# First expert tiles of a fused attention and expert block: numbers in one woven part, weights asked in halves, ScalarE's table loaded ahead

## The chip, the cores and the metric

The kernel runs on one core of a Trainium2 chip. The metric is the device time of one execution in microseconds. The core has five engines that each run their own list of instructions in order: TensorE (PE) for matrix products, VectorE (DVE) and ScalarE (ACT) for work on vectors, GpSimd (POOL) for odd jobs and indirect transfers, and SyncE (SP), which here only issues DMA transfers. The engines wait for each other through semaphores.

## The reference

The input `x` has shape (2, 2048, 256): 4096 tokens. The reference is one block of a network, cut here to what is computed:

```python
# attention: a gated linear recurrence on the normalized input
n   = layernorm(x)
v   = n @ W_write.T                            # 4 heads of 64
rk  = n per head;  wk = rk shifted by one token
# per chunk of tokens: read from the state W, read inside the chunk, write to the state
inter = W @ rk * gamma**p ;  intra = ((rk @ wk.T) * M) @ v
W     = gamma**C * W + (v * g_w).T @ wk
x   = x + n + (alpha * reads) @ W_read.T
# experts: 8 of them, the best two for each token
n   = layernorm(x)
p   = softmax(n @ gate_w.T);  top 2 experts e with weights p_e
h   = gelu(w1[e] @ n + b1[e])                  # 256 -> 1024, tanh approximation
x   = x + sum over e of p_e * (w2[e] @ h + b2[e])
```

## The kernel before

The attention goes in 16 chunks `p` of 128 tokens in both batch rows (`attention(p)`). For each chunk, PE makes `pv` (values and gate columns, line 413), `pS` (products inside the chunk, line 422), `pO` (the result of the chunk before, line 391), the transposes `pt` of the next chunk (line 340), and the reads `pR` (lines 465 and 473) and state writes `pW` (line 493). DVE multiplies `pS` by the mask to give `A` (line 428), adds `pO` to the rows (line 394), updates the state (line 498) and makes `rg` (line 353). ACT copies `pv` to `v` (line 415), scales `wkg` and copies `yT`.

Two chunks make a group `q` of 512 tokens (two chunks in each of the two batch rows), eight groups in all. When a group's rows are done, `route(q)` finds the top two experts of each token and the place in a DRAM table `slots` for it. POOL writes the rows there with eight indirect transfers (`to_slots`). Then `dispatch(q)` finds which experts have a further full tile of 128 rows, and where each such tile starts. Its numbers `t_e` (the expert) and `t_row` (the first row) are computed on DVE by a dozen small operations, in `whole` and around it. `EARLY` fixes the counts: 9 tiles after group 1, 8 after each of groups 2 to 6, and the rest after group 7. 67 tiles run in any case, and four spare ones only if needed.

An expert tile is eight pieces (`piece`). A piece is a product `ph` with a slice of the expert's first weights `w1c` (line 851), a GELU on ACT that gives `hT` (line 856), and three pieces later a product `py` with the second weights, which stay in SBUF (line 813). Before the first piece `prepare` transposes the tile's rows `xg` on PE into `px` (line 787), copies them on DVE to `xT` (line 789), and fetches the bias `b1c`. `px` and `pt` use the same single PSUM buffer with the tag `pt`. `ph` and `pv` use the three buffers `pm`.

SP fetches for a tile the bias row `b2c` (line 755), the weights `w1c` (1 MiB, line 757) and the rows `xg` (line 767). For each it first reads `t_e` or `t_row` into a register (line 746), and so waits until DVE has written it. `w1c`, `b2c` and `xg` have four buffers each.

All engines run in the order in which the Python code issues the instructions. The generators decide the order: `attention(p)` yields at seven steps `k`, and at each the main loop lets `advance` move the routing on. A routing generator that yields `1` asks to be continued by `beside()`, one operation at a time, between the operations of the attention on DVE. A plain `yield` ends its part at this step, and it goes on at the next. Pieces of expert tiles begin in chunk 9 by `pieces_by`.

The main loop asks for weights at each step by `ask_weights_on(stream["piece"] // FC + 2)`, so for the first two tiles as soon as their numbers are known, and at a chunk's end for rows by `ask_on(stream["piece"] // FC + 3)`, so for three tiles. Later, `piece` asks for tile `t + 3` at the second piece of tile `t`.

Of the kernel before, what the change touches and what calls it, by code (L numbers as in the profile page):

```python
# [10 lines left out]
F32 = mybir.dt.float32  # L11
I32 = mybir.dt.int32
AF = mybir.ActivationFunctionType
# [5 lines left out]
P = 128  # L19
B, T, D = 2, 2048, 256  # L20
H, HD = 4, 64
E, F = 8, 1024
# [4 lines left out]
FC = F // P  # L27
# [19 lines left out]
def block_kernel(  # L47
# [16 lines left out]
    nc = tc.nc  # L64
# [11 lines left out]
    def one(shape, dt, name):  # L76
        return keep.tile(shape, dt, name=name)
# [33 lines left out]
    ident = one([P, P], F32, "ident")  # L111
    make_identity(nc, ident)
    nc.gpsimd.memset(ones, 1.0)
    expo = one([P, G], F32, "expo")
    nc.gpsimd.memset(expo, -0.5)
    age = iota(one([P, P], F32, "age"), [[1, P]], -1, -1)
# [105 lines left out]
    def wide(t, k):  # L222
        return t.unsqueeze(2).to_broadcast([P, t.shape[1], k])

    def by_e(t, n):
        return t.unsqueeze(1).to_broadcast([P, n, t.shape[1]])
# [32 lines left out]
    EASY = 9  # L259
    BUSY = 8  # L260
# [266 lines left out]
    def route(q):  # L527
# [105 lines left out]
        yield 1  # L633
        nc.vector.tensor_tensor(pay[:, :, D : D + E], pr, ohs[:, :G], ALU.mult)
        numbers = dispatch(q) if q < NG - 1 else dispatch_rest()
        for k in range(2):
            for i in range(G):
# [9 lines left out]

    tiles, found, known = [], [], []

    def whole(n_f, n, name, ef, row, pick):  # L650

        upto = sml.tile([P, E], F32, tag="upto", name=f"upto_{name}")
        sofar = sml.tile([P, E, E], F32, tag="sofar", name=f"sofar_{name}")
        nc.vector.tensor_tensor(sofar, by_e(n_f, E), not_over, ALU.mult)
        yield 1
        nc.vector.tensor_reduce(upto, sofar, AX.X, ALU.add)
        yield
        origin = sml.tile([P, E], F32, tag="origin", name=f"origin_{name}")
        nc.vector.tensor_tensor(origin, upto, n_f, ALU.subtract)
        yield 1  # L660
        nc.vector.scalar_tensor_tensor(origin, origin, -float(SB), taken, ALU.mult, ALU.add)
        yield 1
        tmp = sml.tile([P, n, E], F32, tag=f"tmp{n}", name=f"tmp_{name}", bufs=1)
        nc.vector.tensor_tensor(tmp, wide(jj[:, :n], E), by_e(upto, n), ALU.is_ge)
        yield 1
        nc.vector.tensor_reduce(ef, tmp, AX.X, ALU.add)
        yield 1
        nc.vector.tensor_tensor(pick, wide(ef, E), by_e(e_of, n), ALU.is_equal)
        yield
        nc.vector.tensor_tensor(tmp, pick, by_e(origin, n), ALU.mult)  # L670
        yield 1
        first = sml.tile([P, n], F32, tag=f"first{n}", name=f"first_{name}", bufs=1)
        nc.vector.tensor_reduce(first, tmp, AX.X, ALU.add)
        yield 1
        nc.vector.scalar_tensor_tensor(row, jj[:, :n], float(SB), first, ALU.mult, ALU.add)

    def dispatch(q):

        n = EARLY[q]
        if not n:  # L680
            return
        n_i = sml.tile([P, E], I32, tag="n_i", name=f"n_i_{q}")
        n_f = sml.tile([P, E], F32, tag="n_f", name=f"n_f_{q}")
        nc.vector.tensor_tensor(n_i, carry[0], taken, ALU.subtract)
        yield 1
        nc.vector.tensor_scalar(n_i, n_i, SB.bit_length() - 1, None, ALU.logical_shift_right)
        yield 1
        nc.vector.tensor_copy(n_f, n_i)
        yield
        t_e = one([P, n], I32, f"t_e_{q}")  # L690
        t_row = one([P, n], I32, f"t_row_{q}")
        hot = one([P, n, E], F32, f"hot_{q}")
        ef = sml.tile([P, n], F32, tag=f"ef{n}", name=f"ef_{q}", bufs=1)
        yield from whole(n_f, n, str(q), ef, t_row, hot)
        nc.vector.tensor_copy(t_e, ef)
        yield
        got = sml.tile([P, E], F32, tag="got", name=f"got_{q}")
        nc.vector.tensor_reduce(got, hot.rearrange("p n e -> p e n"), AX.X, ALU.add)
        yield 1
        nc.vector.scalar_tensor_tensor(taken, got, float(SB), taken, ALU.mult, ALU.add)  # L700
        found.extend((t_e[0:1, j : j + 1], t_row[0:1, j : j + 1], hot[:, j, :], q) for j in range(n))
        known.extend(found)

    def dispatch_rest():
# [14 lines left out]
        nc.vector.tensor_copy(needed, total)  # L719
        ef, row, hot = one([P, NMAX], F32, "ef"), one([P, NMAX], F32, "row"), one([P, NMAX, E], F32, "hot")  # L720
        yield from whole(n_f, NMAX, "rest", ef, row, hot)
        yield

# [17 lines left out]
    stream = {"weights": 0, "asked": 0, "piece": 0, "last": NTILE - SPARE}  # L741
# [3 lines left out]
    def load(src, engine, most):  # L745
        _, (value,) = nc.values_load_multi_w_load_instructions(
            src, [engine], min_val=0, max_val=most, bass_reorder=False
        )
        return value

    def ask_weights(t):

        ev = load(known[t][0], ENG.SP, E - 1)
        b2c = tok.tile([P, D], F32, tag="b2c", name=f"b2c_{t}", bufs=4)
        nc.sync.dma_start(b2c, b2[ds(ev, 1), :].to_broadcast([P, D]))
        w1c = tok.tile([P, 2, F], F32, tag="w1c", name=f"w1c_{t}", bufs=4)
        nc.sync.dma_start(
            w1c.rearrange("p c f -> p (c f)"), w1.rearrange("e p n -> (e p) n")[ds(ev * P, P), :]
        )
        got[t] = (b2c, w1c)  # L760

    def ask(t):

        _, row_at, _, q = tiles[t]
        r0 = load(row_at, ENG.SP, DUMMY)
        xg = tok.tile([P, ROW], F32, tag="xg", name=f"xg_{t}", bufs=4)
        behind(nc.sync.dma_start(xg, next(slot_views)[ds(r0, SB), :]), up_to(q, filled))
        got[t] = (xg, *got[t])

    def ask_weights_on(upto):  # L770
        while stream["weights"] < min(upto, len(known), stream["last"]):
            ask_weights(stream["weights"])
            stream["weights"] += 1

    def ask_on(upto):
        while stream["asked"] < min(upto, len(tiles), stream["last"]):
            ask_weights_on(stream["asked"] + 1)
            ask(stream["asked"])
            stream["asked"] += 1
# [112 lines left out]
    def behind_first():  # L892

        next(setup)
        for c in range(2):
            nc.vector.tensor_scalar(wrg[:, c, :D], wrg[:, c, :D], alpha[:, c : c + 1], None, ALU.mult)
        nc.sync.dma_start(slots[DUMMY : DUMMY + SB, :], empty)
        nc.sync.dma_start(out[N : N + SB, :], empty[:, :D])
        nc.sync.dma_start(b1_sb, b1)

    STEPS = 7
    def advance(whole=True):

        for r in list(routing):
            while inside.get(r) == 1:
                onward(r)
            if r in routing:
                onward(r)
            while whole and inside[r] == 1:
                onward(r)  # L910

    def pieces_by(p, k):


        n = 0.0
        for q, count in enumerate(EARLY):
            share = (p * STEPS + k + 1 - (2 * q + LATE) * STEPS) / (2 * STEPS)
            n += count * FC * min(max(share, 0), 1)
        return int(n)
# [6 lines left out]
    def gate_products():  # L926
# [6 lines left out]
        for m in range(2):  # L933
            nc.vector.tensor_scalar(wrg[:, m, D:], pg[:, m, :], alpha[:, m : m + 1], None, ALU.mult)

    for p in range(NC):
        for k, _ in enumerate(attention(p)):
            if p == 0 and k == 0:
                behind_first()
            if (p or k > 3) and k in (0, 2, 3, 4, 5) and halves < W2_BY[p]:  # L940
                e, j = divmod(halves, 2)
                js = slice(j * FC * D // 2, (j + 1) * FC * D // 2)
                nc.sync.dma_start(w2_sb[:, e, js], w2[e, :, js])
                halves += 1
            if p % 2 == 0 and p and k == 2:
                routing.insert(0, route(p // 2 - 1))
            todo = pieces_by(p, k) - stream["piece"]
            if p < BUSY or not todo:
                advance(p > EASY)
            ask_weights_on(stream["piece"] // FC + 2)  # L950
            for i in range(todo):
                piece()
                if p >= BUSY and (i % 2 == 0 or i == todo - 1):
                    advance()
        if p % 2 and p >= BUSY:
            while routing:
                advance()
        ask_on(stream["piece"] // FC + 3)
    for _ in result(NC - 1):
        piece()  # L960
    routing.append(route(NG - 1))
# [66 lines left out]
```

## Time and profile before

| | |
|---|---|
| median of 3 runs | 642.66 us (640.2 to 644.68) |
| profiled execution | 662.17 us |
| its span, first to last instruction | 660.2 us |
| mean granted clock of TensorE | 0.98 |
| busy: PE, DVE, ACT, POOL | 627.8, 263.3, 287.3, 223.7 us |
| moved by DMA | 129.77 MB |

The profile is of one execution, and its times stand against that execution's own 662.17 us. A group of instructions is named by line, engine, operation and tiles (written tile, arrow, read tiles). In the timeline each row has a start and a length in us; in brackets stands the time that the engine was idle before it, and what ended that. "issue" there means that the profile shows nothing that the engine waited for, "remote" that a semaphore ended the wait and its author isn't known. The chunks can be told by `pv` on PE: chunk 6 begins at 58.92, chunk 7 at 66.47, chunk 8 at 77.57, chunk 9 at 86.81 us.

### The profile page before, as it was taken

How to read it: one execution, taken by the hardware profiler on the slowest of the kernel's cores; microseconds unless marked ns; L12 is line 12 of the kernel's file. 1: busy time of each engine (PE TensorE's matmuls, PEld its weight loads, DVE VectorE, ACT ScalarE, POOL GpSimd, SP SyncE). 2: the span in 40 equal slices, each digit the busy share in tenths (PEclk: the TensorE clock that was granted, in tenths of full speed). 3: DMA queues.
4: the chain of work that ended last, by engine and by line, in shares of the span. 5: the costliest groups of instructions: out<-in, count | busy, mean ns of one | idle time of the engine just before them, and what ended most of it. 6: DMA issues, size and time to landing. Idle time of an engine off the chain costs nothing. (4 is left out here: it accounts for less than half of the span.)

```text
span 660.2 us, 15051 instructions
## 1 busy us (share of the span) xinstructions
PE 627.8 (95%) x4734; PEld 569.2 (86%) x4734; DVE 263.3 (40%) x1138; ACT 287.3 (44%) x769; POOL 223.7 (34%) x199
## 2 busy tenths in 40 slices
PE   7998869899999999999999969999999999999994
PEld 7877659798999898999999959999999999999994
DVE  5788766325543365425542532221122212112220
ACT  6776743334434353434433413444444444444441
POOL 4225483415641165214541551112112211221221
PEclk9999889999999999999999979999999999999998
DMA  4899694866776656677676668767866776666641
GB/s 133 260 332 302 197 319 115 243 177 190 176 215 186 188 151 205 202 192 191 162 203 180 203 198 215 214 184 199 209 205 187 209 215 186 189 225 201 185 99 19
DMA packets 58736, 129.77 MB, mean 197 GB/s; under 512 B 7984, under 2 KB 43952, under 8 KB 50080
## 3 DMA queue, kind: packets, MB, share of 16 engines
q1 hardware_dynamic: 45232, 111.16, 55.6%
q0 software_dynamic: 12720, 17.47, 12.5%
q8 instruction: 42, 0.69, 0.4%
q14 instruction: 38, 0.31, 0.2%
q10 hardware_dynamic: 704, 0.14, 0.1%
HBM read 101.54 MB, written 23.01 MB: 189 GB/s over the span
## 5 line engine op out<-in xcount | busy, mean ns | idle before, releaser
L851 PEld LDWEIGHTS ph<-xT,w1c 128*128 128x128 f32 x2144 | 319.8, 193 | 38.2 <-issue 10.8
L851 PE MATMUL ph<-xT,w1c 128*128 128x128 f32 x2144 | 331.5, 278 | 12.1 <-issue 9.9
L856 ACT ACTIVATE hT<-ph,b1c 128x128 f32<-128x128 f32 x536 | 195.9, 367 | 306.3 <-PE ph L851 278.3
L813 PE MATMUL py<-w_sb,hT 128*128 x1072 | 321.7, 383 | 0.0
L820 POOL DMA_INDIRECT out<-yo,dest x67 | 105.1, 1568 | 328.2 <-DVE dest L803 81.3
L813 PEld LDWEIGHTS py<-w_sb,hT 128*128 128x128 f32 x1072 | 164.2, 193 | 0.2
L819 DVE SCALAR_TENSOR_TENSOR yo<-py,wt,b2c 128x256 f32<-128x256 f32 x67 | 32.3, 483 | 248.7 <-PE py L813 241.7
L521 POOL DMA_INDIRECT slots<-pay,slot_i x64 | 63.4, 990 | 54.6 <-ACT hT L856 19.5
L413 PE MATMUL pv<-wwg,yT 128*128 128x264 f32 x128 | 34.0, 410 | 1.9 <-DVE yT L343 1.2
L391 PE MATMUL pO<-wrg,rdT 128*128 128x264 f32 x128 | 33.3, 393 | 0.4 <-issue 0.4
L428 DVE TENSOR_TENSOR A<-pS,dmask 128x1024 f32<-128x1024 f32 x16 | 19.6, 1224 | 35.3 <-PE pS L422 19.2
L413 PEld LDWEIGHTS pv<-wwg,yT 128*128 128x128 f32 x128 | 24.4, 197 | 6.8 <-DVE yT L343 1.4
L789 DVE COPY xT<-px 128x256 f32<-128x256 f32 x67 | 27.8, 415 | 1.5 <-remote 1.1
L391 PEld LDWEIGHTS pO<-wrg,rdT 128*128 128x128 f32 x128 | 23.6, 190 | 5.1 <-issue 0.8
L394 DVE TENSOR_TENSOR x<-x,pO 128x264 f32<-128x264 f32 x32 | 13.4, 426 | 33.4 <-PE pO L391 30.7
L787 PE MATMUL px<-ident,xg 128*128 128x128 f32 x134 | 25.9, 276 | 0.7 <-ACT yT L346 0.7
L801 DVE TENSOR_SCALAR b2c<-b2c,wt 128x256 f32<-128x256 f32 x67 | 24.9, 372 | 2.5
L787 PEld LDWEIGHTS px<-ident,xg 128*128 128x128 f32 x134 | 18.9, 142 | 7.5 <-ACT yT L346 0.9
L473 PE MATMUL pR<-A,v 128*64 128x128 f32 x256 | 18.6, 279 | 3.1 <-issue 2.2
L232 POOL TENSOR_TENSOR rstd_a<-ve_a,expo 128x2 f32<-128x2 f32 x16 | 13.1, 819 | 23.2 <-DVE ve_a L230 13.7
L422 PEld LDWEIGHTS pS<-yT 64*128 64x128 f32 x256 | 15.5, 187 | 5.8 <-issue 3.8
L551 ACT ACTIVATE pay<-x,shift_b,rstd_b 128x256 f32<-128x256 f32 x32 | 19.0, 594 | 2.4 <-DVE shift_b L237 2.3
(162 smaller groups left out, 431.7 us busy)
## 6 DMA issues: line engine op xcount, KB each, us to landing
w1c<-in_w SPq DMA_DIRECT2D x67, 1024.0 KB
xg<-slots SPq DMA_DIRECT2D x67, 132.5 KB
b2c<-in_b SPq DMA_DIRECT2D x67, 128.0 KB
w_sb<-in_w SPq DMA_DIRECT2D x16, 512.0 KB
out<-x SPq DMA_DIRECT2D x16, 256.0 KB
xin<-in_x SPq DMA_DIRECT2D x15, 256.0 KB
wk<-y SPq DMA_DIRECT2D x16, 224.0 KB
slots<-empty SPq DMA_DIRECT2D x9, 132.5 KB
```

The source lines that it names most:

```text
L391: nc.tensor.matmul(pO, lhsT=rdTs[p][:, c, b * P : (b + 1) * P], rhs=wrg[:, c, :], start=(c == 0), stop=(c == 1))
L413: nc.tensor.matmul(pv, lhsT=yT[:, b, c, 1:], rhs=wwg[:, c, :], start=(c == 0), stop=(c == 1))
L428: nc.vector.tensor_tensor(A, pS.rearrange("p j (b g) -> p j b g", b=B), dmask.rearrange("p j g c -> p j (g c)").unsqueeze(2).to_broadcast( ...
L521: put = nc.gpsimd.indirect_dma_start(out=next(slot_views), out_offset=IndirectOffsetOnAxis(ap=index, axis=0), in_=rows, in_offset=None,)
L787: nc.tensor.transpose(px[:, c, :], xg[:, c * P : (c + 1) * P], ident)
L789: nc.vector.tensor_copy(xT, px)
L801: nc.vector.tensor_scalar(b2c, b2c, wt, None, ALU.mult)
L813: nc.tensor.matmul(r["py"], lhsT=hT, rhs=w2_sb[:, ds(r["at"], 1), fc * D : (fc + 1) * D].rearrange("p a d -> p (a d)"), start=(fc == 0), s ...
L819: nc.vector.scalar_tensor_tensor(yo, r["py"], r["wt"], r["b2c"], ALU.mult, ALU.add)
L820: add = nc.gpsimd.indirect_dma_start(out=next(out_views), out_offset=IndirectOffsetOnAxis(ap=r["dest"], axis=0), in_=yo, in_offset=None, c ...
L851: nc.tensor.matmul(ph, lhsT=r["w1c"][:, c, fc * P : (fc + 1) * P], rhs=r["xT"][:, c, :], start=(c == 0), stop=(c == 1),)
L856: mark[0] = nc.scalar.activation(hT, ph, AF.Gelu_apprx_tanh, bias=r["b1c"][:, fc : fc + 1]).ins.name
```

## The change

There are three edits.

First, `dispatch(q)` and `whole` yield `pause` where they yielded plainly. `pause` is `1` while `2 * (q + 1) < EASY`, so for groups 1 to 3; the numbers of these groups are then issued in one part, one operation at a time beside the attention's, as far as that has places, and the rest at once.

Second, the first two tiles' weights are asked by a generator, `bits`. At each step without pieces it takes one part: the register load and `b2c`, then one half of `w1c`, then the other, and the same for the second tile. While no piece has run, only the rows of two tiles are asked at a chunk's end and not of three.

Third, at step 5 of chunk 7 ACT runs a GELU on one element, so that its table is loaded there.

```diff
+    table = one([1, 1], F32, "table")
...
-    def whole(n_f, n, name, ef, row, pick):
+    def whole(n_f, n, name, ef, row, pick, pause=None):
...
         nc.vector.tensor_reduce(upto, sofar, AX.X, ALU.add)
-        yield
+        yield pause
...
         nc.vector.tensor_tensor(pick, wide(ef, E), by_e(e_of, n), ALU.is_equal)
-        yield
+        yield pause
...
+        pause = 1 if 2 * (q + 1) < EASY else None
...
         nc.vector.tensor_copy(n_f, n_i)
-        yield
+        yield pause
...
-        yield from whole(n_f, n, str(q), ef, t_row, hot)
+        yield from whole(n_f, n, str(q), ef, t_row, hot, pause=pause)
         nc.vector.tensor_copy(t_e, ef)
-        yield
+        yield pause
...
     def ask_weights(t):
 
+        for _ in weights_of(t, 1):
+            pass
+
+    def weights_of(t, parts):
+
         ev = load(known[t][0], ENG.SP, E - 1)
         b2c = tok.tile([P, D], F32, tag="b2c", name=f"b2c_{t}", bufs=4)
         nc.sync.dma_start(b2c, b2[ds(ev, 1), :].to_broadcast([P, D]))
         w1c = tok.tile([P, 2, F], F32, tag="w1c", name=f"w1c_{t}", bufs=4)
-        nc.sync.dma_start(
-            w1c.rearrange("p c f -> p (c f)"), w1.rearrange("e p n -> (e p) n")[ds(ev * P, P), :]
-        )
         got[t] = (b2c, w1c)
+        n = 2 * F // parts
+        for i in range(parts):
+            yield
+            nc.sync.dma_start(
+                w1c.rearrange("p c f -> p (c f)")[:, i * n : (i + 1) * n],
+                w1.rearrange("e p n -> (e p) n")[ds(ev * P, P), i * n : (i + 1) * n],
+            )
...
+    def bits():
+        while not known:
+            yield
+        for t in range(2):
+            stream["weights"] += 1
+            yield from weights_of(t, 2)
+            yield
+
+    first_weights = bits()
     for p in range(NC):
         for k, _ in enumerate(attention(p)):
...
+            if p == BUSY - 1 and k == 5:
+
+                nc.scalar.activation(table, expo[0:1, 0:1], AF.Gelu_apprx_tanh)
...
-            ask_weights_on(stream["piece"] // FC + 2)
+            if stream["piece"] or todo:
+                for _ in first_weights:
+                    pass
+                ask_weights_on(stream["piece"] // FC + 2)
+            else:
+
+                next(first_weights, None)
...
-        ask_on(stream["piece"] // FC + 3)
+        if stream["piece"]:
+            ask_on(stream["piece"] // FC + 3)
+        elif tiles:
+            for _ in first_weights:
+                pass
+            ask_on(2)
```

## The prediction

> **What bounds the kernel now.** I read the busy lines of the page first. TensorE (PE) is busy 627.8 of 660.2 us, so only what keeps PE waiting, or its clock low, counts.
>
> ```profile
> PE 627.8 (95%) x4734; PEld 569.2 (86%) x4734; DVE 263.3 (40%) x1138; ACT 287.3 (44%) x769; POOL 223.7 (34%) x199
> ...
> PEclk9999889999999999999999979999999999999998
> ```
>
> The change works between chunk 6 of the attention and the first expert tiles, so next I cut that stretch into windows (columns: stretch, length, busy of PE, weight loads, DVE, ACT, POOL, then granted clock, DMA share, GB/s).
>
> ```profile
> 74.00:82.00 8.00, 6.17 (x52) 4.80 (x53) 6.10 (x30) 5.67 (x16) 1.22 (x3) 0.79 0.73 231
> 82.00:90.30 8.30, 8.30 (x94) 6.58 (x90) 7.71 (x39) 4.07 (x13) 6.04 (x7) 1.00 1.02 399
> 90.30:96.30 6.00, 0.05 (x2) 0.04 (x1) 1.82 (x4) 2.11 (x6) 5.06 (x5) 0.87 0.97 319
> 96.30:103.50 7.20, 7.20 (x34) 6.84 (x35) 4.22 (x21) 3.87 (x8) 4.37 (x2) 0.63 0.70 186
> ```
>
> PE stands still from 90.3 to 96.3, with the DMA engines full (0.97), and then runs at a clock of 0.63. The timeline tells what it waits for (start, length, engine, operation, idle before it and what ended that).
>
> ```profile
> 73.09 1.04 PE L473 MATMUL pR<-A,v 128*64 128x128 f32 x7
> 75.97 0.74 PE L473 MATMUL pR<-A,v 128*64 128x128 f32 x9 [1.83 <-issue]
> ...
> 89.88 0.44 PE L787 MATMUL px<-ident,xg 128*128 128x128 f32 x2
> 93.40 1.23 DVE L428 TENSOR_TENSOR A<-pS,dmask 128x1024 f32<-128x1024 f32 x1 [3.03 <-remote]
> 95.78 0.42 DVE L789 COPY xT<-px 128x256 f32<-128x256 f32 x1 [1.06 <-remote]
> 96.27 2.93 PE L851 MATMUL ph<-xT,w1c 128*128 128x128 f32 x12 [5.95 <-issue]
> 97.10 1.28 ACT L856 ACT_TABLE_LOAD   x1 [4.69 <-DVE cw L797]
> 98.98 0.63 PE L787 MATMUL px<-ident,xg 128*128 128x128 f32 x2
> ```
>
> The first `ph` waits for `xT`, which stands on DVE behind `A` of chunk 9. `A` starts 3.5 us after its last `pS` matmul (89.9) and is put down to nothing known ("remote"). So the first tile waits for a release that came late while the DMA engines were full, and not plainly for its weights: `px` had already read tile 0's rows at 89.88.
>
> How much of that is in the timed runs? The profiled execution took 662.17 us (span 660.2), 19.5 more than the median of 642.66. Adding up PE's waits over 0.3 us in the timeline gives 23.7 us, and the half-speed stretches (mean clock 0.980) cost some 7.7 more: 31.4. So about 12 of 31 us, 38%, can be left in a timed run, and some 6 of these are plain waits such as the first 1.45. The halt at 75.97 lies inside one run of 16 matmuls whose inputs were ready, so some halts follow no dependence. I make the sum against the profiled execution and carry only the difference to the median.
>
> **The table of ScalarE.** One load moves from the first GELU to ahead of `v` of chunk 8; the count of loads stays one and a 1x1 activation (0.2 by the 0.18 of ACT's smallest copy) comes on. Removed: 1.28 (the row). At full clock three `ph` take 1.3 us and `px` 0.2, and the fourth needs a buffer of `pm` that the first GELU frees; with the load that GELU ends 2.5 us after the first `ph`, so 0.95 us shows. At the half clock of this trace almost none does (`px` at 98.98, GELU done at 98.76). Value -0.95, bounds 0 and -1.28. Added at the new place: 1.5 us before `v` at 80.56, which `pR` needs at 85.3; `wkg` and `yT` come later by as much, and `yT` waited 1.83 for PE anyway. Cost 0; without that slack 1.5.
>
> **The numbers in one part.** For groups 1 to 3 the dispatch's operations no longer leave the steps' places; the built order shows them on DVE all before the additions of `pO`. The same operations run, but dependent ones now follow each other directly:
>
> ```profile
> 60.05 0.22 DVE L620 TENSOR_TENSOR oh<-oh,cnt 128x64 f32<-128x64 f32 x1
> 60.31 0.22 DVE L623 TENSOR_REDUCE slot<-oh 128x8 f32<-128x64 f32 x1
> ...
> 87.71 0.15 DVE L329 TENSOR_TENSOR std<-ve_a,rstd_a 128x2 f32<-128x2 f32 x1
> 87.82 0.22 DVE L673 TENSOR_REDUCE first<-tmp 128x8 f32<-128x64 f32 x1
> ```
>
> A dependent successor starts 0.26 after its predecessor, an independent one 0.11. Laying chunk 8's operations from `n_f` (84.30) to `rg` in the new order with these spacings, `rg` starts at 89.65 instead of 89.00: +0.65 per dispatch. Is DVE on the path there? From `A` of chunk 6 (62.09) its work back to back is 7.96 + 9.35 + 7.95 us for chunks 6, 7 and 8, so `A` of chunk 9 can start at 87.35. PE without its 2.3 us of halts and the slow `pv` (3.71 for 2.05) would end `pS` at 85.9. So DVE is late: `ph` could start at 89.2 and PE idles 2.9 us even with no late release. Chunks 6 and 8 lie on this path: 2 x 0.65 = +1.3 (bounds 0, if releases on PE come last as in the trace, and 2.6, twice the spacing).
> For group 3 the numbers go ahead of `xT` of tile 2. They take 2.8 us on DVE from 111.2, so `xT` ends at 114.45 rather than 111.6. The transposes `pt` of chunk 10 share the one PSUM buffer `pt` with `px` and stand at 113.45 on PE: a wait of +1.0 (bounds 0 and 2.0). Behind them stand all of PE's queue. `rstd_b` on POOL starts 1.6 us later, its reader `pL` comes after the same numbers: 0. POOL's second put of a dispatch goes behind `rstd_a` (0.72 us); the last put began at 73.52 and `xg` was asked at 79.08: 0, and 0.7 if that slack is gone.
>
> **The weights in halves.** What SP asks, in the trace of before:
>
> ```profile
> 70.59 0.52 SPq L309 DMA_DIRECT2D wk<-y  x1
> ...
> 75.98 0.34 SPq L757 DMA_DIRECT2D w1c<-in_w  x1
> ...
> 79.08 1.47 SPq L767 DMA_DIRECT2D xg<-slots  x2
> 81.36 0.34 SPq L755 DMA_DIRECT2D b2c<-in_b  x1
> ```
>
> Now tile 0's `b2c` and `w1c` come before chunk 6's last write of `out`, tile 1's `b2c` before `wk` of chunk 8, its halves after `xin`; `xg` of 0 and 1 follow, and tile 2 is asked only in chunk 9. SP waits for `t_e` on DVE, and behind that wait stand `out`, three `wk` and one `xin`. A tile's `b2c` and `w1c` take SP 2.6 us (74.52 to 77.14), so `wk` is up to 4 us later; `wkg` reads it at 81.65, 9.6 us after 72.0: hidden, and 4 us if not. Two more issues of 0.34 us each: hidden.
> The Trainium skill speaks against halves ("DMA: Bandwidth & Descriptors", Bandwidth): batch transfers to 1 MiB or more; by its fit for GpSimd's queue (Anatomy of one DMA) each carries a fixed 2 us, so two more would be +4 us of loading. The row of 82.0 to 90.3 has 399 GB/s with several transfers in flight: the fixed part overlaps. By the row 0, and even 4 us fit in the 13 us between the request at 75.98 and the first `ph`. I take 0, and for the range -7 to +4.
> What it may bring: 3 MB no longer stand in one burst at 82 to 96. If all of the late release (3.43 + 1.06 = 4.5 us) and the slow clock after it go, that is most of the 5.95. Of the loss in this place beyond DVE's own 2.9 (5.95 + half of 6.8 us slow clock less the part PE stood in, 2.65, less 2.9 = 5.7), 38% or 2.2 us is in a timed run, and I let half go: -1.1.
> On the clock the skill ("TensorE: Matmul & The Clock Gate", Part 1) wants an idle window of about 3.4 us before the clock halves. By it DVE's 2.9 us costs nothing and 4.2 might cost 1.7 (half of one window). The row says otherwise: halts of 0.47 and 1.83 us already preceded the 0.79 of 74 to 82. So both kernels may pay, and I put no difference in.
>
> Sum: -0.95 + 1.3 + 1.0 - 1.1 = +0.25, so 642.9.
>
> **The rivals.** *The gap is the weights' and goes.* For it: full DMA engines exactly there. Against it: `px` ran at 89.88, and halts elsewhere have no such burst. It gives -4.5 - 2.65 - 0.95 + 1.3 = -6.8: 635.9.
> *Tile 2 comes late (slower).* Its first DMA is asked where tile 3's was before. That one began its register load at 93.9, issued `w1c` at 96.48 and `xg` at 97.26, behind which 1.3 MB at 186 GB/s take 7 us: rows at 103.5 to 104. `px` of tile 2 is 11 pieces of 0.88 us and 2.2 us of attention after the first `ph`. With that `ph` at 89.2 it is due at 101, so PE waits 3.0, and one slow stretch as in the trace (6.83 us at half speed) adds 3.4; with +2.3 and -0.95 it makes +7.7: 650.4. It decides from an `xg` over 2 us later than its `px`. Against it: without halts SP is earlier by the same 4 us, and then `xg` lands near 99.5.
> *Nothing moves but the table*: the release comes late in both; -0.95 and +1.0: 642.7, inside the forecast.
>
> **How the numbers follow.** Forecast with the third rival 0.54, weights 0.22, tile 2 late 0.24. One per cent (6.4 us) is about what a measurement of this kernel can tell from no change; the forecast's own cases run from 638.5 (-4.2) to 646.5 (+3.6). The range takes in the middle of both other cases, 634.5 to 651. Faster 0.22, same 0.53, slower 0.25.
>
> **What would show it.** Right: the table load near 79 to 81, the first GELU right after `b1c`; `A` of chunk 9 and `xT` on DVE ending PE's wait for the first `ph`; `pt` of chunk 10 waiting for `xT`. Wrong: no wait at all before the first `ph` and a full clock after it (weights), or a wait of `px` of tile 2 on `xg` of some us. I would be wrong altogether if the halts of PE came from the profiling alone and none were left.

## The result and the profile after

| | before | after |
|---|---|---|
| median | 642.88 us (639.55 to 645.89, 20 runs) | 646.13 us (642.89 to 648.24, 20 runs) |
| profiled execution, span | 662.17, 660.2 us | 645.42, 643.5 us |
| mean granted clock of that execution | 0.98 | 0.994 |

The ratio is 1.0046, with a 95% interval of 1.0026 to 1.0065: 3.0 us slower, 1.7 to 4.2. That is inside "within 1%", but it isn't the +0.25 us of the sum.

The two profiled executions can't be subtracted. That of before holds halts of TensorE (stops that no wait explains) that are not in that of after, and the runs below show that such halts come on some chips and not on others: the unchanged kernel took 643.15 us on one chip, 655.95 and 660.28 us on two more. So each experiment is compared with the kernel before on its own chip, and waits are read from stretches of traces without halts.

First the page of the changed kernel, the busy line of TensorE (PE) and its clock in 40 slices.

```profile
PE 620.6 (96%) x4734; PEld 563.1 (88%) x4734; DVE 264.9 (41%) x1138; ACT 288.4 (45%) x770; POOL 224.1 (35%) x199
...
PEclk9999999999999999999999998999999999999998
```

The same windows as before (columns: stretch, length, busy of PE, weight loads, DVE, ACT, POOL, then granted clock, DMA share, GB/s):

```profile
74.00:82.00 8.00, 6.28 (x52) 4.49 (x49) 7.42 (x34) 6.62 (x17) 2.83 (x4) 1.00 0.87 291
82.00:90.30 8.30, 6.81 (x82) 5.32 (x80) 7.82 (x38) 5.45 (x15) 5.96 (x7) 1.00 0.75 221
...
90.30:96.30 6.00, 5.23 (x37) 4.95 (x38) 4.85 (x24) 3.73 (x11) 5.36 (x4) 1.00 0.73 189
96.30:103.50 7.20, 7.20 (x51) 6.59 (x50) 4.64 (x23) 2.30 (x7) 4.54 (x4) 1.00 0.95 335
```

The clock is full in all of them, the long stop is gone, and DVE is the busiest engine in the second window (7.82 of 8.30 us). PE's timeline shows where PE waits now:

```profile
72.39 0.67 PE L466 MATMUL pR<-rg,state 64*64 64x128 f32 x16 [0.84 <-DVE A L429]
78.17 1.13 PE L414 MATMUL pv<-wwg,yT 128*128 128x264 f32 x4 [1.01 <-DVE state L499]
85.86 2.02 PE L414 MATMUL pv<-wwg,yT 128*128 128x264 f32 x8 [0.52 <-DVE x L395]
88.90 0.44 PE L799 MATMUL px<-ident,xg 128*128 128x128 f32 x2
91.07 1.60 PE L863 MATMUL ph<-xT,w1c 128*128 128x128 f32 x12 [1.74 <-DVE xT L801]
101.98 0.43 PE L799 MATMUL px<-ident,xg 128*128 128x128 f32 x2
106.67 0.66 PE L341 MATMUL pt<-ident,y 128*128 128x128 f32 x4 [0.74 <-DVE xT L801]
```

Every wait here ends on DVE, none on a transfer. (Between them stand two shorter ones: 0.53 us for DVE before the counts `pK` at 75.51, and 0.17 us for `v` of ACT at 81.66.) `px` of tile 2 (101.98) doesn't wait, so the slower rival, tile 2 late, did not happen. DVE's own rows for the chain of `A` are these:

```profile
61.61 1.22 DVE L429 TENSOR_TENSOR A<-pS,dmask 128x1024 f32<-128x1024 f32 x1
68.94 0.68 DVE L354 TENSOR_TENSOR rg<-yT,g_p 128x512 f32<-128x512 f32 x1
70.57 0.19 DVE L547 TENSOR_TENSOR pL<-x,rstd_b 128x32 f32<-128x32 f32 x1 [0.79 <-POOL rstd_b L233]
71.12 1.22 DVE L429 TENSOR_TENSOR A<-pS,dmask 128x1024 f32<-128x1024 f32 x1
...
88.81 0.19 DVE L547 TENSOR_TENSOR pL<-x,rstd_b 128x32 f32<-128x32 f32 x1
89.36 1.22 DVE L429 TENSOR_TENSOR A<-pS,dmask 128x1024 f32<-128x1024 f32 x1
90.60 0.42 DVE L801 COPY xT<-px 128x256 f32<-128x256 f32 x1
```

No `A` waits for PE: DVE sets the pace from chunk 6 to the first tile. The step from `A` of chunk 6 to that of chunk 7 takes 9.51 us, and inside it is a wait that the prediction had put at nothing: `pL` stands 0.79 us for `rstd_b` of POOL.

### The profile page after: what moved, and what is told of

Same layout as the page of the kernel before. It is cut to its first block, busy times and chain, and to the rows that moved or that the text cites. A ratio compares the mean times of both kernels' runs of the same rounds, so it can differ in the third digit from the quotient of the medians.

```text
span 643.5 us, 15055 instructions
## 1 busy us (share of the span) xinstructions
PE 620.6 (96%) x4734; PEld 563.1 (88%) x4734; DVE 264.9 (41%) x1138; ACT 288.4 (45%) x770; POOL 224.1 (35%) x199
## 5 line engine op out<-in xcount | busy, mean ns | idle before, releaser
L423 PE MATMUL pS<-yT 64*128 64x128 f32 x256 | 18.6, 284 | 0.0
```

What stands on the lines that cost most here:

```text
L423: nc.tensor.matmul(pS[:, j, (2 * b + hh) * P : (2 * b + hh + 1) * P], lhsT=yT[r, b, hh, 0:P], rhs=yT[r, b, hh, 1:], start=True, stop=True,)
```

## The experiments

### The edits one by one

Four kernels ran on one chip, where the kernel before took 655.95 us. The first is the kernel before itself.

> The kernel before once more, nothing changed: a control for the size of a difference that means nothing, and a second profile of it. All theories: ratio within 0.998 to 1.002. If the long halts of PE in the first profile of before came with that one execution, this profile has a span near 641 us, no late release of A in chunk 9, and PE waits before the first ph for xT alone, by some 2 to 3 us.

Measured: 1.0009 (0.9982 to 1.0036). In this trace of the unchanged kernel no halt holds the first `ph` (rows of DVE and PE, then the second GELU on ACT and the fifth `ph`):

```profile
82.31 1.22 DVE L428 TENSOR_TENSOR A<-pS,dmask 128x1024 f32<-128x1024 f32 x1 [2.77 <-PE pS L422]
90.19 1.22 DVE L428 TENSOR_TENSOR A<-pS,dmask 128x1024 f32<-128x1024 f32 x1
91.42 0.42 DVE L789 COPY xT<-px 128x256 f32<-128x256 f32 x1
91.89 1.60 PE L851 MATMUL ph<-xT,w1c 128*128 128x128 f32 x12 [2.55 <-DVE eq L571]
94.04 0.71 PE L851 MATMUL ph<-xT,w1c 128*128 128x128 f32 x4 [0.33 <-ACT hT L856]
...
96.18 0.62 ACT L856 ACTIVATE hT<-ph,b1c 128x128 f32<-128x128 f32 x2 [1.71 <-PE ph L851]
96.60 0.71 PE L851 MATMUL ph<-xT,w1c 128*128 128x128 f32 x4 [1.42 <-ACT hT L856]
```

`A` of chunk 9 starts with no idle time, 7.88 us after that of chunk 8, `xT` follows, and then `ph`. PE waits 2.55 us there for DVE's order alone, where the prediction had 2.9. The fifth `ph` then stands 1.42 us for a GELU that ACT began 1.71 us after its last operation, although the product it reads was done by 93.49 (91.89 + 1.60). No trace from the chip without halts has that wait, so I count it as a halt and not as a cost of the order.

The table alone:

```diff
+    table = one([1, 1], F32, "table")
...
+            if p == BUSY - 1 and k == 5:
+                nc.scalar.activation(table, expo[0:1, 0:1], AF.Gelu_apprx_tanh)
```

> Before, with the load of ScalarE's table in chunk 7 and nothing else changed. My theory: -0.95 us from the first GELU, ratio near 0.9985, and the table load hidden in chunk 8. Rival (the load costs at its new place, because v of chunk 8 comes 1.5 us later and DVE or PE then wait): ratio 1.001 to 1.004.

Measured: 1.0016 (0.9989 to 1.0042). A gain of 0.95 us would be 0.9985; the interval holds neither that nor a loss over 2.8 us.

The numbers alone (the first edit):

```diff
+        pause = 1 if 2 * (q + 1) < EASY else None
...
-        yield
+        yield pause
```

> Before, with the numbers of groups 1 to 3 in one woven part and nothing else changed (the first tiles' weights are then asked as early as the numbers allow, in one piece). My theory: DVE is late by 0.65 us in each of chunks 6 and 8 and pt of chunk 10 waits for xT by 1.0: +2.3 us, ratio near 1.0036. Rival (the loss of the changed kernel is from its transfers): ratio 1.000.

Measured: 1.0089 (1.0059 to 1.0119), +5.8 us. It is the only one of the four that differs from no change.

The weights alone (`bits`, halves and two tiles' rows; `pause` left at `None`, no early table):

```diff
-            ask_weights_on(stream["piece"] // FC + 2)
+            if stream["piece"] or todo:
+                for _ in first_weights:
+                    pass
+                ask_weights_on(stream["piece"] // FC + 2)
+            else:
+                next(first_weights, None)
```

> Before, with the first two tiles' weights asked in halves at the steps' places and tile 2 asked only in chunk 9, and nothing else changed. My theory: hidden, -1 to 0 us, ratio 0.9985 to 1.000. Rival (tile 2's rows come too late, or the transfers collide): px of tile 2 waits for xg, ratio 1.003 to 1.006.

Measured: 0.9997 (0.9973 to 1.002), which is -1.8 to +1.3 us. No difference is shown; the -1.1 us of the prediction lies in the interval as well as 0, and more transfers cost at most 1.3 us.

### Which group's numbers, and the rest without them

Four kernels on a second chip, where the kernel before took 660.28 us. The first is the changed kernel.

> The changed kernel with all three edits, beside the runs below on one chip. My theory: the numbers in one part cost, the other two edits do next to nothing, and so the whole is what the numbers cost: ratio 1.003 to 1.009 to the kernel before. Rival, weights in halves mend part of what the numbers cost: ratio 1.000 to 1.004 here, and well under numbers without the other two edits (1.0089 on another chip).

Measured: 0.9967 (0.9943 to 0.9992). On this chip the changed kernel is a little faster. The second undoes the first edit in it:

```diff
-        pause = 1 if 2 * (q + 1) < EASY else None
+        pause = None
```

> The changed kernel with edit 1 undone: the numbers of all groups leave the steps' places again; weights in halves and the early table stay. My theory (only the numbers cost): ratio 0.997 to 1.001 to the kernel before, -0.95 us of the table at most visible. Rival, the loss is from transfers asked at other times: the ratio stays over 1.002.

Measured: 1.0013 (0.9989 to 1.0037). The two remaining edits together give nothing that these intervals can show, as they did alone. The other two run the numbers in one part in the kernel before, for some groups only:

```diff
+        pause = 1 if q in (1, 2) else None
```

> The kernel before, with the numbers in one part for groups 1 and 2 alone (chunks 6 and 8). By the prediction's step (0.65 us later A, twice): +1.3 us, ratio 1.002. By what the run of the numbers alone showed (evictions of pO wait behind the numbers on DVE, and pv behind these, +1 to +5 us): ratio 1.003 to 1.008. Rival, all of the loss is from group 3 and the transposes of chunk 10: ratio 1.000.

```diff
+        pause = 1 if q == 3 else None
```

> The kernel before, with the numbers in one part for group 3 alone (chunk 10). By the prediction's step (pt of chunk 10 waits for xT of tile 2): +1.0 us, ratio 1.0015, between 1.000 and 1.003, and the wait is to be seen at pt of chunk 10. Rival, all of the loss is from groups 1 and 2: ratio 1.000 and no wait there.

Measured: 1.004 (1.0002 to 1.0078) for groups 1 and 2, and 0.9979 (0.9954 to 1.0004) for group 3. The trace for group 3 has the predicted wait, on `pt` of chunk 10, where the kernels with the old order have none:

```profile
112.64 0.66 PE L340 MATMUL pt<-ident,y 128*128 128x128 f32 x4 [0.78 <-DVE xT L790]
```

Its time on this chip doesn't show it. PE loses more here than the effect in question. In the trace without the numbers, for example, it stops twice inside `pR`, whose inputs the profile shows as there:

```profile
77.33 0.27 PE L474 MATMUL pR<-A,v 128*64 128x128 f32 x1 [1.60 <-issue]
78.77 0.27 PE L474 MATMUL pR<-A,v 128*64 128x128 f32 x1 [1.18 <-issue]
```

### All edits, numbers alone, and old requests, on a chip without halts

Four kernels ran on a third chip, where the kernel before took 643.15 us. First the changed kernel, and the numbers alone.

> The changed kernel with all three edits, beside the numbers alone (next run) on one chip. Theory A, the edits act together (spread requests mend what earlier numbers cost): ratio 0.996 to 1.002 here and at least 0.004 below the next run. Theory B, only the numbers matter and earlier differences were those of chips: this run and the next differ by under 0.002.

> The numbers in one part for groups 1 to 3 alone, weights and table as before. Theory A: ratio 1.005 to 1.010 again, with 2 MB of weights asked before chunk 8's transfers of y and x. Theory B: as the run of all three edits on this chip, within 0.002. By the prediction's sum (+1.3 and +1.0 us): 1.0035.

Measured: 1.0048 (1.0033 to 1.0063) and 1.0045 (1.0028 to 1.0063). The two times are the same, as theory B says: the numbers alone lose as much as all three edits, 2.9 us (1.8 to 4.1) of 643.15. The sum of the prediction had +2.3 for them.

The trace of the numbers alone has something that the changed kernel doesn't have. With the numbers known earlier, SP asks for both tiles' weights ahead of `out`, and ACT waits for `out` before it can write `x` again (rows of ACT and PE):

```profile
80.77 1.09 ACT L321 ACTIVATE x<-xin,shift_a,up 128x256 f32<-128x256 f32 x2 [5.15 <-DMA out<-x]
83.53 1.86 PE L391 MATMUL pO<-wrg,rdT 128*128 128x264 f32 x4 [2.35 <-ACT v L415]
...
93.62 1.60 PE L852 MATMUL ph<-xT,w1c 128*128 128x128 f32 x12 [1.39 <-DVE xT L790]
93.72 1.28 ACT L857 ACT_TABLE_LOAD   x1 [0.86 <-DVE b1c L794]
95.02 0.37 ACT L857 ACTIVATE hT<-ph,b1c 128x128 f32<-128x128 f32 x1
95.44 0.71 PE L852 MATMUL ph<-xT,w1c 128*128 128x128 f32 x4
```

The same wait of `x` for `out` is in the two kernels with early numbers and whole weights on the other chips (2.61 and 3.86 us), and in none of the others. So the steps of `bits` do avoid a wait, but one that only the first edit brings. In the time of these two kernels it hardly shows. The first `ph` starts 32.28 us after `A` of chunk 6 here and 29.43 in the changed kernel on this chip, 2.85 us later. But near 390 us, where every trace of the kernels on this chip has a wait of `px` for its rows `xg`, the numbers alone wait 2.17 us and the changed kernel 2.98, and behind it only the changed kernel runs a stretch at half clock, which costs 1.7 us. Is the wait for `out` what the numbers cost? The next kernel takes it away by asking at the step of the kernel before:

```diff
+        pause = 1 if 2 * (q + 1) < EASY else None
...
-            ask_weights_on(stream["piece"] // FC + 2)
+            if p != 6 or k >= 4:
+                ask_weights_on(stream["piece"] // FC + 2)
```

> The numbers in one part for groups 1 to 3, but the first two tiles' weights are asked at the same step as in the kernel before (step 4 of chunk 6), behind chunk 6's transfers and not ahead of them. If the cost of the numbers is in DVE's order (pO's evictions late, pv behind them, pt behind xT): as the numbers alone, 1.005 to 1.010. If it is the requests that come earlier and stand before y and x: 1.000 to 1.0035, what the DVE order itself costs (pv +1.0, pt +0.8 us by the traces).

Measured: 1.0076 (1.0053 to 1.0098). The wait for `out` is gone, and the loss is not (4.9 us, 3.4 to 6.3). What PE waits for in this trace is DVE's order, with no halt among it:

```profile
71.70 0.67 PE L465 MATMUL pR<-rg,state 64*64 64x128 f32 x16 [0.83 <-DVE A L428]
...
86.76 2.02 PE L413 MATMUL pv<-wwg,yT 128*128 128x264 f32 x8 [0.96 <-DVE x L394]
...
91.96 1.60 PE L852 MATMUL ph<-xT,w1c 128*128 128x128 f32 x12 [1.72 <-DVE xT L790]
```

The first `ph` waits 1.72 us here with whole weights, and 1.72 us in the changed kernel on the same chip with halves. A stretch at half clock, in which `pv` and `pS` of chunk 8 end 1.6 us late, comes on top in this trace.

### `xT` of the first tile ahead of `A`

If DVE's order holds the first `ph`, moving `xT` ahead should free it. The kernel before with the early table and this:

```diff
+            if p == BUSY and k == 4:
+                coming.append(prepare(0))
+                next(coming[0])
+                next(coming[0])
```

> The kernel before with the early table, and px, xT and b1c of tile 0 issued at step 4 of chunk 8, so ahead of pL and A of chunk 9 on DVE. My theory (the first ph waits for DVE's order): the wait before the first ph falls from 2.55 us to under 1 us; the fourth ph then waits about 1 us for hT, since v and pay stand on ACT till about 92.3; together -1.3 us, ratio 0.998. Rival: DVE's order isn't what holds the first ph (a late release or w1c): the wait stays over 2 us, ratio 1.000.

Measured: 1.0048 (1.0031 to 1.0064), slower and not faster. The wait before the first `ph` is gone, but others took its place (rows of SP and PE):

```profile
79.86 1.48 SPq L768 DMA_DIRECT2D xg<-slots  x2
...
86.44 0.41 PE L788 MATMUL px<-ident,xg 128*128 128x128 f32 x2 [1.98 <-DMA xg<-slots]
87.57 2.04 PE L414 MATMUL pv<-wwg,yT 128*128 128x264 f32 x8 [0.72 <-DVE xT L790]
90.63 1.60 PE L852 MATMUL ph<-xT,w1c 128*128 128x128 f32 x12
```

`px` now stands ahead of `pv` of chunk 9, and the rows `xg`, asked only at 79.86, aren't there. PE loses 1.98 + 0.72 us in front of the attention's next chunk, in place of the wait behind it. By this trace's own rows the old order would have had `px` behind `pS`: `pW` ends at 84.46, `pv` and `pS` take 3.13, so `pS` ends at 87.6. `A` and `xT` then end 1.65 later, and the first `ph` starts at about 89.3, 1.3 us before 90.63. So 1.3 of the 3.1 us are shown; for the rest, the granted clock of its runs was 0.991 on average where that of before was 0.9935, which is 1.6 us of span, and why isn't settled.

Up to chunk 8 this kernel issues the old order on DVE, PE and POOL. So it also serves as a halt-free view of it. (The 1.60 us before its first row here are of a stretch at half clock, in which `pS` took 2.08 us and not 1.16.) Its `A` chain, and POOL's queue in both kernels (first this one, DVE and POOL; then the changed kernel, POOL):

```profile
62.38 1.22 DVE L429 TENSOR_TENSOR A<-pS,dmask 128x1024 f32<-128x1024 f32 x1 [1.60 <-PE pS L423]
65.83 1.04 POOL L522 DMA_INDIRECT slots<-pay,slot_i  x1 [0.20 <-issue]
67.47 1.04 POOL L233 TENSOR_TENSOR rstd_b<-ve_b,expo 128x4 f32<-128x4 f32 x1 [0.60 <-DVE ve_b L231]
69.77 0.18 DVE L547 TENSOR_TENSOR pL<-x,rstd_b 128x32 f32<-128x32 f32 x1
70.32 1.22 DVE L429 TENSOR_TENSOR A<-pS,dmask 128x1024 f32<-128x1024 f32 x1
```

```profile
65.51 1.04 POOL L522 DMA_INDIRECT slots<-pay,slot_i  x1 [0.41 <-issue]
66.86 0.96 POOL L522 DMA_INDIRECT slots<-pay,slot_i  x1 [0.30 <-issue]
68.12 0.96 POOL L522 DMA_INDIRECT slots<-pay,slot_i  x1 [0.30 <-issue]
69.11 1.43 POOL L233 TENSOR_TENSOR rstd_b<-ve_b,expo 128x4 f32<-128x4 f32 x1
```

In the old order one put of `slots` stands between `rstd_a` and `rstd_b` on POOL, and `A` follows `A` after 7.94 us. In the new order three stand there, `rstd_b` ends at 70.54, and DVE waits for it.

## Why the prediction was right and wrong

The forecast of a time within 1% held, and 646.13 lies in the range. The signs named for "right" came too: the table load at 79.85, `A` and `xT` on DVE ahead of the first `ph`, and `pt` of chunk 10 waiting for `xT`. But the number came out of a sum whose gains weren't seen and whose largest cost was half of what it is. Each miss was under 2 us and the range reached 8 us to either side, so that the hit says little for the sum.

| step | predicted, us | shown, us |
|---|---|---|
| table | -0.95 | 0 to -0.33 |
| numbers, chunk 6 (`A` to `A`: 7.94 to 9.51) | +0.65 | +1.57 |
| chunk 7 (9.25 to 9.32) | 0 | +0.07 |
| numbers, chunk 8 (7.88 to 8.92) | +0.65 | +1.04 |
| `pt` of chunk 10 | +1.0 | +0.74 to +0.78 |
| weights | -1.1 | 0 at the first `ph`; in the time -1.8 to +1.3 |
| sum, weights at 0 | +0.25 | +3.1 to +3.5; measured +3.0 (1.7 to 4.2) |

The `A` steps of the old order are from intervals in which no `A` waited for PE: the early-`xT` kernel for chunks 6 and 7, the kernel before run again for chunk 8. Of the seven traces with these numbers early, five give 9.50 to 9.51 for chunk 6. The other two, from the chip with the most halts, give 9.30 and 9.32, made up otherwise: `state` on DVE waits 0.59 and 0.60 us for PE just before, and `rstd_b` (1.04 us there, not 1.43) is done when `pL` comes.

**What bounds the kernel.** Right in kind: DVE's order holds the first `ph` in the kernel before (2.55 us when it was run again), and its steps of 7.96, 9.35 and 7.95 us measured 7.94, 9.25 and 7.88. The 2.9 us of waiting was too much for a chip without halts. There DVE would be ready for `A` of chunk 9 at 79.57 + 7.88 = 87.45 by the early-`xT` trace, and `pS` ends at 87.6: both come together. `px` ends at about 88.0 and the first `ph` can start at 89.3, so about 1.3 us of waiting are left. So nearly all of the DVE delay that the numbers add is exposed.

**The numbers.** The mechanism was right, and so nearly was the size of the spacing: +0.65 was predicted from `n_f` to `rg`, and the traces show 4.78 to 5.46 us in chunk 6, which is +0.68, and 4.72 to 5.55 in chunk 8, +0.83. The step that failed outright is the sentence that `rstd_b` on POOL starts 1.6 us later and costs 0. In chunk 6 it starts 7.50 us after `A` and not 5.09, so 2.4 later. It followed `rstd_b` against its reader on DVE, and of POOL's queue only the second put against `rstd_a`; it did not count the puts between `rstd_a` and `rstd_b`. There are two more of them, and DVE stands 0.79 us: from `rg` to `A` it takes 2.18 us and not 1.29, +0.89. In chunk 8 `rstd_b` ends at 88.77 and `pL` starts at 88.81, and `rg` to `A` takes 1.50 us, +0.21. So of the 2.6 us in chunks 6 and 8, 1.5 are DVE's spacing and 1.1 POOL's queue. The waits that PE then has (0.84 at `pR` of chunk 7, for `A`, and 0.52 at `pv` of chunk 9, for an eviction of `pO`) had no place in the sum, which looked only at the first `ph`. By this reading they don't add to it: they are the same delay on its way.

**`pt` of chunk 10.** Right: +1.0 predicted, 0.74 to 0.78 shown, in all seven traces with group 3's numbers early and in none without.

**The table.** The step that failed is that the first GELU ends 2.5 us after the first `ph`. In the row above the load begins 0.10 us after that `ph` begins, long before it ends: the profile has it wait for `b1c` of DVE, and not for `ph`. So the GELU ended 1.77 us after it, and the fourth `ph`, behind three `ph` and a `px` of 1.82 us together, waited for nothing; in the kernel before run again, where ACT still had a `pay` to write and began the load 0.44 us after the first `ph`, it waited 0.33. The cost at the new place, put at 0, was 0.17 us: in the changed kernel the second `pO` of chunk 8 waits so long for `v`.

**The weights.** The term let half of 2.2 us of late release go. In the traces without halts there is no late release at the first tile, with whole weights as with halves. Where releases do come late, the edit alone gives 0.9997 (0.9973 to 1.002), too wide to rule the term out. Against the fixed 2 us for each transfer of the Trainium skill ("DMA: Bandwidth & Descriptors", Anatomy of one DMA, there for GpSimd's queue), the row was the better guide: two more transfers, +4 us by the estimate, cost nothing that these intervals can show.

**The clock.** No difference was put in. On the third chip the clock took 5.1 us of the span on average with the changed kernel and 4.2 with that before (span times one less the mean clock), so at most 0.9 of the 3.1 us is the clock's. That leaves 2.2 us, less than the sum of the waits. The numbers alone, with 3.4 us of clock and 2.9 of loss, leave 3.6, and with the old requests (6.0 and 4.9) 3.0. The three come from 15, 6 and 6 executions, too few to tell them apart.

**Two slips of the working.** 642.66 + 3.6 is 646.3 and not 646.5, and the sum of the first rival leaves out the +1.0 of `pt`. No conclusion rests on them.

**What stays open.** On the chip with the most halts the changed kernel was faster (0.9967) and on the one between them the numbers alone cost 5.8 us, more than their waits add up to. DVE's delays can hide behind halts of PE that come at the same time, or bring more of them; that is argued, no run separates it, and what causes the halts wasn't tried. The shares of DVE's spacing and of POOL's queue are read from traces: no run moved `rstd_b` alone. And a delay at the first tile isn't paid in full for certain: the wait of `px` near 390 us ran from 2.17 to 3.38 us in the five traces without halts, and no trace of the unchanged kernel without halts shows what it was there.

## What to carry to other kernels

When operations move on one engine, write out the queue of every engine that reads or feeds them, item by item: here two transfers issued by POOL slipped in front of a small operation that DVE was waiting for, and in chunk 6 cost more (0.89 us) than the reordering itself (0.68). A wait that goes away gives nothing until what is late next is known, as the early `xT` shows. And a cost taken from one execution with halts belongs to that chip; compare the intervals between the same instruction in successive chunks, which for the old order came out at 7.94 us in three kernels on two chips.

## What the runs showed of the hardware

The unchanged kernel took 643.15, 655.95 and 660.28 us on three chips. The longer times go with a lower mean clock (0.9935, 0.985, 0.982) and with stops of PE in the middle of runs of matmuls.

Stretches of half clock come in lengths of 3.41, 6.83 and 10.24 us in these traces, apart from one at the very end of each. A wait of 1.72 us before the first `ph` was followed by one in one trace of the changed kernel, while 1.74 us in another was not. At the wait near 390 us 2.98, 3.19 and 3.38 us were followed by one, 2.17 and 2.90 were not; and in the early-`xT` kernel one came behind two waits of only 0.61 and 0.77 us. "TensorE: Matmul & The Clock Gate" of the Trainium skill (Part 1) asks for an idle window of about 3.4 us; here shorter waits were followed by half clock at times, and the length of a single wait doesn't decide.

ACT's load of a table took 1.28 us, began before the product that its activation reads was finished, and was followed by the activation at once (93.72 + 1.28, then 95.02).
